# Stage projections in column tiles of 32 outputs and a second convolution in tiles of 32 by 64

## The chip, the cores and the metric

The kernel runs on one core of one Trainium2 chip. The metric is the time of one execution on the device in microseconds; it stood at 2982.66 us (median of three runs) before the change. Below, PE is TensorE, DVE is VectorE, ACT is ScalarE, POOL is GpSimd and SP is SyncE. A "pass" is one matmul record of the trace: an f32 matmul of this kernel is recorded as two.

## What is computed

The input is x with 2 images of 256 channels on 64 by 64 points, all in f32. Two layers follow each other. In short:

```python
# layer 0: full attention over 4096 tokens, 8 heads of 32, and a fusion with a mask
q, k, v = proj(Wq) / sqrt(32), proj(Wk), proj(Wv)
fuse = softmax(q @ k.T) @ v
hybrid = conv1x1(concat([x, fuse]), Wf) + bf
x = hybrid * m + x * (1 - m)
# layer 1: channel gate, window attention (8x8 windows, 4 heads of 64), two grouped 7x7 convolutions
a = relu(xp @ ca_w1 + ca_b1) @ ca_w2 + ca_b2
x = x * sigmoid(a)
q, k, v = split(windows(x) @ qkv_w + qkv_b)
x = x + (softmax(q @ k.T * 64**-0.5) @ v) @ out_w + out_b
x = shuffle(x, groups=4)
y = relu(bn(conv7x7(x, sa_w1, groups=64)))
y = bn(conv7x7(y, sa_w2, groups=64))
return x * sigmoid(y)
```

## The kernel before

A first part projects q, k and v and puts them into DRAM. Then `pipeline` runs, and nearly all of the time is spent there. One of two arms is taken at run time; the one in the profile has the suffix "a" on its tiles.

**The main loop** (lines 1177 to 1201) goes through 1024 slots: 2 images, 8 chunks of 512 queries, 2 groups of 4 heads, 32 blocks of 128 keys. A slot issues, in this order:

- `scores(i + 2)`: 8 matmuls of 32 rows by 64 columns on 512 queries (L633), into PSUM, and exponentials on ACT (L646);
- `products(i)`: 4 matmuls of 128 rows by 32 columns that accumulate the weighted values (L665), and on DVE one add of 128 x 2048 elements that sums the exponentials (L667). The first slot of a group of heads has no add;
- actions that fell due (`run_later`): at the end of a chunk come the denominators (L688, 128 rows by 32 columns), a reciprocal on DVE (L721), its spread over the heads on PE (L704) and a multiply (L724);
- at every fourth slot one piece of `stage`.

[...] The exponentials have 8 buffers, so PE and ACT can run ahead of DVE by some slots.

**The stage** (lines 728 to 989) does all the rest of a chunk of 512 tokens, in pieces that are spread over the slots of the next chunk. Its matmuls, with their form before the change (rows * columns of the array) and the recorded passes of one stage:

| line | what | form | passes |
|---|---|---|---|
| L739 | fusion of x and attention, 512 wide | 128*128 | 16 |
| L768 | first product of the channel gate, 256 wide | 128*64 | 8 |
| L782 | second product of the gate | 64*128 | 8 |
| L810 | query and key projections, twice | 128*128 | 8 each time |
| L844 | window scores, twice | 64*64 | 32 each time |
| L896 | value projection, 256 wide | 128*128 | 16 |
| L919, L938 | window probabilities transposed, window products | 64*64 | 64 each |
| L960 | output projection | 128*128 | 8 |

Between them ACT moves results out of PSUM and DVE does the multiplies and adds (L751, L753 after the fusion, L856 and L877 for the window softmax, L971 at the end). They stand in the same queues as the exponentials and the adds of the main loop. The stage of a chunk ends with its rows stored to DRAM for the convolutions.

**The convolutions** (`convolve`, lines 999 to 1151) run at the end, the first of them between the pieces of the last stage. They have 24 items: 16 "narrow" ones that treat one image (192 wide) and 8 "wide" ones that treat both (384 wide). For each item there is `conv1(k + 1)` (L1052, 28 matmuls of 128 rows by 32 columns), `conv2(k)` (L1076, 28 matmuls of 32 rows by 128 columns, in two PSUM pairs), two tanh on ACT (L1086) and a scaling (L1092) into `z`, which has two buffers, and `gate(k)`: one multiply on DVE (L1098) and 12 or 24 stores to the output (L1111). The stores go to POOL's and SP's queues in turn. For the items below 8 they all go to POOL once the last stage is done. The convolution weights live in the buffers of the exponentials, and SP loads them.

Of the kernel before, what the change touches and what calls it, by code (L numbers as in the profile page):

```python
# [17 lines left out]
B, C, H, W = 2, 256, 64, 64  # L18
# [19 lines left out]
KS, PAD = 7, 3  # L38
# [5 lines left out]
HALVES = (slice(0, 64), slice(64, 128))  # L44
# [12 lines left out]
def conv_seq_kernel(ctx: ExitStack, tc: tile.TileContext, a, out):  # L57
    nc = tc.nc
# [13 lines left out]
    def psum2(name):  # L72
        return ps["pair"].tile([P, 2, CH], F32, tag="s", name=name)
# [299 lines left out]
    with (  # L373
# [48 lines left out]
        for i, (b, c) in enumerate(chunks):  # L422
            load_chunk()
            x = xs0[i]
            sq = st0.tile([P, 2 * KC, CH], F32, tag="sq", name=f"sq_{b}_{c}")
            tops = st0.tile([P, 2 * KC, CH // 4], F32, tag="top4", name=f"top4_{b}_{c}")
            for n, w in (("q", wq), ("k", wk)):
                s = psum2(f"{n}0_{b}_{c}")
                for g in range(KC):
                    for kc in range(KC):  # L430
                        rhs = x[:, kc, :]
                        if n == "q":
# [5 lines left out]
                            start=(kc == 0),  # L438
                            stop=(kc == KC - 1),
# [26 lines left out]
        for i, (b, c) in enumerate(chunks):  # L466
            s = psum2(f"v0_{b}_{c}")
            sv = s.rearrange("p a (t o) -> p (a t) o", t=2)
            for m in range(4):
                for kc in range(KC):  # L470
# [4 lines left out]
                        start=(kc == 0),  # L475
                        stop=(kc == KC - 1),
# [21 lines left out]
            elif i == 2:  # L498
# [3 lines left out]
                for oc in range(KC):  # L502
                    for kc in range(KC):
# [4 lines left out]
                            start=(kc == 0),  # L508
                            stop=(kc == KC - 1),
# [10 lines left out]

    def pipeline(arm, shifted, pools):
        fp, xpool, gp, wp, avp, ctx_conv = pools
        cpool = ctx_conv.enter_context(tc.tile_pool(name=f"conv{arm}", bufs=1))
# [202 lines left out]
        def stage(b, c):  # L728
            x, f = xts.pop((b, c)), fts.pop((b, c))
# [6 lines left out]
            for half in range(2):  # L736
                for oc in range(KC):
                    for kc in range(KC * half, KC * half + KC):
                        nc.tensor.matmul(  # L739
                            s[:, oc, :],  # L740
                            wf[:, kc, oc * P : (oc + 1) * P],
                            f[:, kc - KC, :] if half else xw[kc],
                            start=(kc == 0),
                            stop=(kc == 2 * KC - 1),
                        )
# [19 lines left out]
            s = psum2(f"ca1{tag}")  # L765
            for kc in range(KC):
                for h in range(2):
                    nc.tensor.matmul(  # L768
                        s[64 * h : 64 * h + 64, 0, 0:half],
                        cw1[:, kc, :],  # L770
                        x1[:, kc, toks[h]],
                        start=(kc == 0),
                        stop=(kc == KC - 1),
                    )
# [4 lines left out]
            for oc in range(KC):  # L779
                for h in range(2):  # L780
                    r = slice(64 * h, 64 * h + 64)
# [4 lines left out]
                        start=True,  # L786
                        stop=True,
# [17 lines left out]
            def project(hc):  # L805
                s = psum2(f"qk{tag}_{hc}")
                for j in range(2):
                    o = (KC * j + hc) * P
                    for kc in range(KC):
                        nc.tensor.matmul(  # L810
                            s[:, j, :],
                            wqkv[:, kc, o : o + P],
                            u[:, kc, :],
                            start=(kc == 0),
                            stop=(kc == KC - 1),
                        )
                return s
# [56 lines left out]
            def normalise(hc):  # L874
                e, rs = es_[hc], sums[hc]
                nc.vector.reciprocal(rs, rs)
                nc.vector.tensor_mul(e, e, rs.unsqueeze(2).to_broadcast([P, 8, 64]))  # L877

            project_out(0, project(0))
            yield True  # L880
            window_scores(0)
            yield

            s = project(1)
            window_exp(0)
            project_out(1, s)
# [6 lines left out]
            sv = s.rearrange("p a (t o) -> p (a t) o", t=2)  # L893
            for t in range(4):
                for kc in range(KC):
                    nc.tensor.matmul(  # L896
                        sv[:, t, :],
                        u[:, kc, t * P : (t + 1) * P],
                        wqkv[:, kc, 2 * C : 3 * C],
                        start=(kc == 0),  # L900
                        stop=(kc == KC - 1),
                    )
# [9 lines left out]
            for hc in range(KC):  # L912
                for h in range(2):
                    for tt in range(2):
                        for odd in range(2):
                            for w in range(2):
                                r = slice(64 * w, 64 * w + 64)
# [5 lines left out]
                                    start=True,  # L923
                                    stop=True,
# [6 lines left out]
            o = s.rearrange("p w (a t q) -> p w a t q", a=KC, t=4)  # L931
            for hc in range(2):
                for t in range(4):
                    for w in range(2):
                        for h in range(2):
                            n = 2 * hc + h
                            r = slice(64 * w, 64 * w + 64)
# [4 lines left out]
                                start=True,  # L942
                                stop=True,
# [13 lines left out]
            y = gp.tile([P, KC, CH], F32, tag="t", name=f"y{tag}")  # L957
            for oc in range(KC):
                for kc in range(KC):
                    nc.tensor.matmul(  # L960
                        s[:, oc, :],
                        wo[:, kc, oc * P : (oc + 1) * P],
                        ots[kc],
                        start=(kc == 0),
                        stop=(kc == KC - 1),
                    )
# [32 lines left out]
        def convolve():  # L999
# [12 lines left out]
            weights = deque([*range(1, NU), 1])  # L1012
# [54 lines left out]
            def conv2(k):  # L1067
                u, images = items[k]
                n = nb * len(images)
                y = ys.pop(k)  # L1070
                w = ws[u][:, 32 * UW :].rearrange("p (m d) -> p d m", d=KS)
                tiles = [psum2(f"c2{arm}{k}_{hh}") for hh in range(2)]
                for d in range(KS):
                    for j in range(4):
                        r = slice(32 * j, 32 * j + 32)
                        nc.tensor.matmul(  # L1076
                            tiles[j // 2][:, j % 2, 0 : n * W],
                            w[r, d],
                            y[r, 0:n, d : d + W],
                            start=(d == 0),  # L1080
                            stop=(d == KS - 1),
                        )
                z = pool.tile([P, 4, B * nb * W], F32, tag="z", name=f"z{arm}{k}", bufs=2)
                z = z[:, :, 0 : n * W]
                for hh in range(2):
                    nc.scalar.activation(  # L1086
                        z[:, 2 * hh : 2 * hh + 2, :],
                        tiles[hh][:, :, 0 : n * W],
                        AF.Tanh,
                        scale=0.5,  # L1090
                    )
                nc.scalar.activation(z, z, AF.Copy, bias=0.25, scale=0.25)  # L1092
                return z.rearrange("p j (n x) -> p j n x", x=W)
# [42 lines left out]
            for k, (u, images) in enumerate(items):  # L1136
                while len(xs) <= k + 1 < len(items):
                    if not more():
                        yield
                conv1(k + 1)  # L1140
                yield
                more()
                z = conv2(k)
                yield
                more()
                gate(k, z)
                if xcs or k + 4 < EARLY:
                    load_rows(k + 4)

                if weights and (weights[0] <= 1 + EB or k >= EARLY):  # L1150
                    load_w(weights.popleft())
# [25 lines left out]
        for i, (b, c, g, m) in enumerate(slots):  # L1177
            now[0] = i
            if (b, c, g, m) == (B - 1, NCHUNK - 1, 0, 0):
                for _ in banded:  # L1180
                    pass
                conv = convolve()
                next(conv)
            if m % PB == 0:
                load_piece(i // PB + AHEAD)
            if g == KC - 1 and m == 0:
                nxt = (b, c + 1) if c + 1 < NCHUNK else (b + 1, 0)
                if nxt[0] < B:
                    load_q(*nxt)
            rest = scores(i + 2) if i + 2 < len(slots) else None  # L1190
            products(i)
            if rest:
                rest()
            if g == KC - 1 and m == NMB - 1:
                late = EB + 5 if (b, c) == (0, 0) else 0
                at(DN + 6 + late, lambda b=b, c=c: stages.append(stage(b, c)))
            run_later()
            if i % 5 == 1:
                next(banded, None)
            if i % 4 == 0:  # L1200
                run_stages()
# [20 lines left out]
    def arm(name, shifted):  # L1222
        with (
            tc.tile_pool(name=f"f{name}", bufs=1) as fp,
            tc.tile_pool(name=f"x{name}", bufs=1) as xpool,
            tc.tile_pool(name=f"g{name}", bufs=1) as gp,
            tc.tile_pool(name=f"w{name}", bufs=1) as wp,
            tc.tile_pool(name=f"av{name}", bufs=1, space=PSUM) as avp,
            ExitStack() as ctx_conv,
            tc.manual_schedule(),  # L1230
        ):
            pipeline(name, shifted, (fp, xpool, gp, wp, avp, ctx_conv))
# [71 lines left out]
```

## Time and profile before

| | us |
|---|---|
| median of three runs (2981.29 to 2983.53) | 2982.66 |
| the profiled execution | 2982.11 |
| its span, first to last instruction | 2980.3 |
| PE busy | 2942.5 |
| DVE busy | 2504.0 |
| ACT busy | 2474.1 |
| POOL busy | 267.1 |

The granted TensorE clock was 0.996 of full speed. The page's chain of waits, which is followed back from the last instruction, gives 87% of the span to PE, 34% of it to L633, 32% to L665; 6% to DVE; 2% each to the DMAs, ACT and POOL. The PE matmul groups that the change touches are busy for 118.4 us (L810), 116.7 us (L739, in two groups), 99.7 us (L1076), 59.5 us (L896), 59.2 us (L960) and 17.8 us (L768).

How to read the lines that follow: a group has the line of the source, the engine, the operation, what is written and read, the tile of the array (rows * columns) and the shape, then how many; behind the bar the busy time in us and the mean of one in ns, then the idle time of the engine before them and what ended it. A timeline line has the start and the duration in us first, and in brackets the idle time before it. Matmuls are pipelined and their ends are modelled, so the distance from one start to the next says more than a duration. A wait for several semaphores is put down to the one that came last.

### The profile page before, as it was taken

How to read it: one execution, taken by the hardware profiler on the slowest of the kernel's cores; microseconds unless marked ns; L12 is line 12 of the kernel's file. 1: busy time of each engine (PE TensorE's matmuls, PEld its weight loads, DVE VectorE, ACT ScalarE, POOL GpSimd, SP SyncE). 2: the span in 40 equal slices, each digit the busy share in tenths (PEclk: the TensorE clock that was granted, in tenths of full speed). 3: DMA queues.
4: the chain of work that ended last, by engine and by line, in shares of the span. 5: the costliest groups of instructions: out<-in, count | busy, mean ns of one | idle time of the engine just before them, and what ended most of it. 6: DMA issues, size and time to landing. Idle time of an engine off the chain costs nothing.

```text
span 2980.3 us, 77927 instructions
## 1 busy us (share of the span) xinstructions
PE 2942.5 (99%) x33674; PEld 928.1 (31%) x33674; DVE 2504.0 (84%) x1348; ACT 2474.1 (83%) x4151; POOL 267.1 (9%) x470
## 2 busy tenths in 40 slices
PE   9999999999999999999999999999999999999997
PEld 3551222222222222222222222222222222222775
DVE  4349999899999999999999999999999999999211
ACT  5569879898989898998989898989899898989433
POOL 8110000000000000000000000000000000000366
PEclk9999999999999999999999999999999999999998
DMA  8545322222242323232222223222323232322474
GB/s 247 198 166 171 119 70 52 78 67 70 54 80 63 81 63 69 72 75 70 65 70 67 70 53 74 63 74 62 68 74 73 68 73 68 101 66 86 128 215 103
DMA packets 224018, 267.12 MB, mean 90 GB/s; under 512 B 113384, under 2 KB 130108, under 8 KB 223408
## 3 DMA queue, kind: packets, MB, share of 16 engines
q1 hardware_dynamic: 200880, 231.47, 27.2%
q0 software_dynamic: 18416, 27.87, 4.6%
q8 instruction: 267, 4.37, 0.6%
q10 hardware_dynamic: 4368, 2.70, 0.3%
q14 instruction: 87, 0.71, 0.1%
HBM read 213.49 MB, written 66.13 MB: 94 GB/s over the span
## 4 chain that ended last, share of the span: by engine, by line
PE 87%; DVE 6%; DMA 2%; ACT 2%; POOL 2%; issue 1%; SPq 1%; DVEq 0%; ACTq 0%
PE sa L633 34%; PE ava L665 32%; DVE suma L667 5%; PE qka L810 4%; PE hya L739 4%; PE vwa L896 2%; PE opa L960 2%; PE v L471 2%; PE q L434 2%; POOL out_dram L1111 2%; PE k L434 1%; DMA out_dram<-za 1%; ACT ea L646 1%; PE sca L844 1%; PE rda L704 1%
## 5 line engine op out<-in xcount | busy, mean ns | idle before, releaser
L667 DVE TENSOR_TENSOR suma<-suma,ea 128x2048 f32<-128x2048 f32 x960 | 2198.8, 2290 | 87.9 <-ACT ea L646 1.4
L646 ACT ACTIVATE ea<-sa 128x512 f32<-128x512 f32 (+1 forms) x3072 | 2038.4, 745 | 74.3 <-PE sa L633 35.8
L633 PE MATMUL sa<-qa,ka 32*64 32x512 f32 x16384 | 1167.4, 613 | 1.5 <-ACT vst L479 1.2
L665 PE MATMUL ava<-ea,va 128*32 128x512 f32 x8192 | 1091.9, 605 | 1.3 <-ACT fa L675 0.3
L633 PEld LDWEIGHTS sa<-qa,ka 32*64 32x64 f32 x16384 | 251.4, 129 | 763.2 <-ACT ea L646 696.9
L665 PEld LDWEIGHTS ava<-ea,va 128*32 128x32 f32 x8192 | 161.6, 108 | 835.1 <-issue 806.2
L986 POOL DMA_DIRECT2D xs<-xo x94 | 65.9, 708 | 2524.0 <-DVE xo L971 2523.8
L1111 POOL DMA_DIRECT2D out_dram<-za x210 | 117.8, 569 | 74.3 <-DVE za L1098 51.3
L810 PE MATMUL qka<-ua,qkv_w 128*128 128x512 f32 x256 | 118.4, 605 | 0.0
L667 DVE TENSOR_TENSOR suma<-ea,ea 128x2048 f32<-128x2048 f32 x32 | 73.0, 2283 | 51.3 <-ACT ea L646 51.3
L1098 DVE TENSOR_TENSOR za<-za,xla 128x768 f32<-128x768 f32 (+1 forms) x16 | 21.7, 1359 | 108.2 <-ACT za L1092 60.1
L1076 PE MATMUL c2a<-yca,wa 32*128 32x192 f32 (+1 forms) x1344 | 99.7, 438 | 3.1 <-ACT za L1086 3.1
L453 DVE TENSOR_REDUCE top<-sq 128x512 f32<-128x2048 f32 x16 | 36.6, 2285 | 77.7 <-ACT sq L447 77.7
L1086 ACT ACTIVATE za<-c2a 128x384 f32<-128x384 f32 (+1 forms) x48 | 26.1, 595 | 90.8 <-DMA out_dram<-za 70.7
L747 ACT ACTIVATE ta<-hya,bf 128x512 f32<-128x512 f32 x32 | 20.3, 684 | 95.4 <-PE hya L739 89.2
L1076 PEld LDWEIGHTS c2a<-yca,wa 32*128 32x128 f32 x1344 | 90.9, 315 | 13.7 <-issue 9.6
L865 ACT ACTIVATE ewa<-ewa,mxwa 128x64 f32<-128x64 f32 x256 | 85.2, 346 | 1.5 <-DVE mxwa L856 1.5
L823 ACT ACTIVATE qka<-qka,qkv_b 128x512 f32<-128x512 f32 x64 | 40.5, 683 | 42.1 <-PE qka L810 41.7
L810 PEld LDWEIGHTS qka<-ua,qkv_w 128*128 128x128 f32 x256 | 46.0, 189 | 71.3 <-issue 46.1
L751 DVE TENSOR_TENSOR ta<-ta,mca 128x512 f32<-128x512 f32 x32 | 22.0, 688 | 54.5 <-ACT ta L747 54.5
L434 PE MATMUL q<-x,WqT 128*128 128x512 f32 x128 | 60.6, 617 | 5.1 <-DMA WqT<-in_WqT_dram 5.1
L896 PE MATMUL vwa<-qkv_w,ua 128*128 128x256 f32 x256 | 59.5, 386 | 0.0
(137 smaller groups left out, 1516.0 us busy)
## 6 DMA issues: line engine op xcount, KB each, us to landing
ka<-ks SPq DMA_DIRECT2D x256, 256.0 KB
va<-vs SPq DMA_DIRECT2D x256, 256.0 KB
wa<-ws SPq DMA_DIRECT2D x17, 896.0 KB
ws<-zeros SPq DMA_DIRECT2D x16, 896.0 KB
xs<-xo POOLq DMA_DIRECT2D x78, 140.0 KB, 6.3
xla<-xs SPq DMA_DIRECT2D x24, 420.0 KB
x<-in_x_dram SPq DMA_DIRECT2D x16, 512.0 KB
qs<-qst SPq DMA_DIRECT2D x16, 512.0 KB
```

The lines of the kernel that those rows point to most:

```text
L434: nc.tensor.matmul(s[:, g, :], w[:, kc, g * P : (g + 1) * P], rhs, start=(kc == 0), stop=(kc == KC - 1),)
L633: nc.tensor.matmul(heads[j][o], k[r, cols][:, o], q[r, g, :], start=True, stop=not shifted)
L646: nc.scalar.activation(e[:, h, :], tile, AF.Exp, scale=SCALE0)
L665: nc.tensor.matmul(av[r, :], v[:, m % PB, r], e[:, j, :], start=start, stop=stop)
L667: nc.vector.tensor_add(total, first[0] if m == 1 else total, e)
L739: nc.tensor.matmul(s[:, oc, :], wf[:, kc, oc * P : (oc + 1) * P], f[:, kc - KC, :] if half else xw[kc], start=(kc == 0), stop=(kc == 2 * K ...
L810: nc.tensor.matmul(s[:, j, :], wqkv[:, kc, o : o + P], u[:, kc, :], start=(kc == 0), stop=(kc == KC - 1),)
L865: nc.scalar.activation(e[:, n, :], e[:, n, :], AF.Exp, bias=mx[:, n : n + 1], accum_out=rs[:, n : n + 1],)
L896: nc.tensor.matmul(sv[:, t, :], u[:, kc, t * P : (t + 1) * P], wqkv[:, kc, 2 * C : 3 * C], start=(kc == 0), stop=(kc == KC - 1),)
L986: eng.dma_start(x_s[b, n, p + r0 : p + r1].rearrange("r g w -> g r w"), xo[64 * h : 64 * h + 64, oc, r0 - WS * c : r1 - WS * c, :],)
L1076: nc.tensor.matmul(tiles[j // 2][:, j % 2, 0 : n * W], w[r, d], y[r, 0:n, d : d + W], start=(d == 0), stop=(d == KS - 1),)
L1111: engines[stores % len(engines)].dma_start(dst[b, i, r0:r1, UG * u : UG * u + UG, :], z[p + r0 : p + r1, :, nb * m + n, :],)
```

## The change

Six matmul sites change, and nothing else does. A new helper splits the weights (the stationary operand) into tiles of 32 columns, and with them the output rows in PSUM; each tile streams the same x. It replaces the matmul call in the fusion (L739), the first gate product (L768), the projections (L810, L896) and the output projection (L960). In the second convolution each matmul of 32 rows by 128 columns becomes two of 32 rows by 64 columns; `HALVES` is the pair of slices 0 to 64 and 64 to 128. The elements that are multiplied and the order in which each output accumulates stay as they are.

```diff
+    def by_columns(out, weights, x, start, stop):
+        for o in range(0, weights.shape[-1], 32):
+            nc.tensor.matmul(
+                out[o : o + 32], weights[:, o : o + 32], x, start=start, stop=stop
+            )
...
-                        nc.tensor.matmul(
+                        by_columns(
                             s[:, oc, :],
                             wf[:, kc, oc * P : (oc + 1) * P],
                             f[:, kc - KC, :] if half else xw[kc],
...
-                    nc.tensor.matmul(
+                    by_columns(
                         s[64 * h : 64 * h + 64, 0, 0:half],
                         cw1[:, kc, :],
                         x1[:, kc, toks[h]],
...
-                        nc.tensor.matmul(
+                        by_columns(
                             s[:, j, :],
                             wqkv[:, kc, o : o + P],
                             u[:, kc, :],
...
-                    nc.tensor.matmul(
+                    by_columns(
                         sv[:, t, :],
                         u[:, kc, t * P : (t + 1) * P],
                         wqkv[:, kc, 2 * C : 3 * C],
...
-                    nc.tensor.matmul(
+                    by_columns(
                         s[:, oc, :],
                         wo[:, kc, oc * P : (oc + 1) * P],
                         ots[kc],
...
-                        nc.tensor.matmul(
-                            tiles[j // 2][:, j % 2, 0 : n * W],
-                            w[r, d],
-                            y[r, 0:n, d : d + W],
-                            start=(d == 0),
-                            stop=(d == KS - 1),
-                        )
+                        for o in HALVES:
+                            nc.tensor.matmul(
+                                tiles[j // 2][o, j % 2, 0 : n * W],
+                                w[r, d, o],
+                                y[r, 0:n, d : d + W],
+                                start=(d == 0),
+                                stop=(d == KS - 1),
+                            )
```

## The prediction

> **What bounds the kernel now.** I read the page first: busy shares, then the costliest groups.
>
> ```profile
> span 2980.3 us, 77927 instructions
> PE 2942.5 (99%) x33674; PEld 928.1 (31%) x33674; DVE 2504.0 (84%) x1348; ACT 2474.1 (83%) x4151; POOL 267.1 (9%) x470
> L667 DVE TENSOR_TENSOR suma<-suma,ea 128x2048 f32<-128x2048 f32 x960 | 2198.8, 2290 | 87.9 <-ACT ea L646 1.4
> L1076 PE MATMUL c2a<-yca,wa 32*128 32x192 f32 (+1 forms) x1344 | 99.7, 438 | 3.1 <-ACT za L1086 3.1
> ```
>
> PE is busy for 99%, but its ends are modelled, so I count from start to start. The second thing to see is VectorE: one softmax add takes 2.29 us, more than the PE needs for a slot. The timeline of PE around two stage pieces gives all prices:
>
> ```profile
> 1479.13 1.06 PE L665 MATMUL ava<-ea,va 128*32 128x512 f32 x8
> 1480.01 1.93 PE L688 MATMUL dna<-suma,keysum 128*32 128x128 f32 x64
> 1481.87 1.11 PE L633 MATMUL sa<-qa,ka 32*64 32x512 f32 x16
> ...
> 1534.45 1.06 PE L665 MATMUL ava<-ea,va 128*32 128x512 f32 x8
> 1535.44 3.70 PE L810 MATMUL qka<-ua,qkv_w 128*128 128x512 f32 x8
> 1539.08 1.11 PE L633 MATMUL sa<-qa,ka 32*64 32x512 f32 x16
> 1540.12 1.06 PE L665 MATMUL ava<-ea,va 128*32 128x512 f32 x8
> 1541.12 1.11 PE L633 MATMUL sa<-qa,ka 32*64 32x512 f32 x16
> ```
>
> A slot is 1.04 us of scores (tiles 32*64) and 1.00 us of products (128*32): 2.04 us. The products take 1.00 us before a group in another tile shape (1540.12 to 1541.12), and 0.88 us before the denominators, which have the same shape (1479.13 to 1480.01). So a change of shape costs about 0.115 us. An f32 matmul is two recorded passes; eight passes of L810 take 3.64 us, sixteen of L739 7.07 us (1501.82 to 1508.89), so a full-array pass is 0.429 us and a piece has 0.21 us of fixed cost.
>
> The timeline of weight loads at the start of L739 shows half of that cost: the second pass comes 0.54 us after the first (1501.82), the third 0.43 us after the second.
>
> ```profile
> 1502.36 0.19 PEld L739 LDWEIGHTS hya<-xa,WfT 128*128 128x128 f32 x1 [0.24 <-issue]
> 1502.79 0.19 PEld L739 LDWEIGHTS hya<-xa,WfT 128*128 128x128 f32 x1 [0.24 <-issue]
> ```
>
> Then VectorE's timeline in one chunk period (161.5 us), for who waits for whom:
>
> ```profile
> 1509.71 0.69 DVE L751 TENSOR_TENSOR ta<-ta,mca 128x512 f32<-128x512 f32 x1 [3.51 <-ACT ta L747]
> 1549.22 0.69 DVE L856 TENSOR_REDUCE mxwa<-ewa 128x8 f32<-128x512 f32 x1 [0.17 <-ACT ewa L852]
> 1552.14 16.67 DVE L667 TENSOR_TENSOR suma<-suma,ea 128x2048 f32<-128x2048 f32 x7
> 1569.81 0.69 DVE L856 TENSOR_REDUCE mxwa<-ewa 128x8 f32<-128x512 f32 x1 [1.00 <-ACT ewa L852]
> ```
>
> and PE's at the one place where it waits for VectorE:
>
> ```profile
> 1648.36 0.56 PE L704 MATMUL rda<-inva,spread_h 32*64 32x128 f32 x12 [0.82 <-DVE inva L721]
> ```
>
> Seven adds in 16.67 us are 2.39 us each: VectorE is slower than PE's slot and idles only three times a period. Call these points A (DVE waits for the fusion, 3.51 us), B (waits for the second window scores, 1.00 us) and C (PE waits for VectorE's reciprocal of L721, 0.5 to 0.8 us). From A to B, and from C to the next A, PE decides; from B to C VectorE runs without a real gap, and what PE wins there only lengthens its wait at C.
>
> [...] the denominators' 64 passes take 1.86 us; less one change of shape that is 0.109 us for a round of four 32-column tiles streaming 128 elements, beside 0.107 us that 0.429 us for 512 elements gives.
>
> **The change, part by part.** *Stage pieces.* Each full-array pass becomes four passes of 32 columns that run side by side, so the streaming time stays: 16 rounds of 0.429 for L739, 8 for each L810 and for L960, 16 of 0.216 for L896 (256 wide), 4 of 0.216 for L768, which already had two column tiles and two passes per tile. PE gets some 2,800 more matmul passes and as many loads, hidden: eight instructions fall in 0.43 us, and L919 issues 64 of each in 1.09 us. What goes is the change of shape ahead of the piece, since the products before it have shape 128*32 too (0.115 us), and the exposed first load (about 0.09 us net). The change towards the scores behind it remains. So L739, each L810, L896 and L960 win 0.20 us, L768 0.15 us (it had 64-column loads). Whole stage: 1.15 us.
>
> Which of this arrives? Between A and B lie L768 and both L810: 0.55 us. At B VectorE's 1.00 us gap shrinks to about 0.6 and still exists, so all 0.55 arrives; 14 periods (chunks 2 to 15) give 7.7 us. Between C and A lies L739: 0.20 us, 13 periods, 2.6 us. L896 and L960 lie between B and C: 0.40 us per period turns into a longer wait at C and counts nothing. Were VectorE not in the way, they would add 13 x 0.4 = 5 us. Chunk 0 has no stage; the fusion of the first stage falls where VectorE is the bound (adds every 2.39 us, full exp buffers). The rest of that stage and the fusion after it precede the first real wait A: 4 x 0.20 + 0.20 = 1.0 us. After the last B nothing of VectorE is late, so L896 and L960 count: 0.4 us. Sum in the loop: 11.7 us. The last stage runs among convolutions, where first-convolution neighbours have shape 128*32 as well; with the same prices about 1.0 us.
>
> *Second convolution.* The tail's timeline gives 3.51 us for 56 passes 192 wide and 4.90 us for 384 wide. The difference is 0.099 us a round, but 192 elements at L810's rate need 0.161 us. So the narrow form waits for its loads of 128 columns: a round is 0.24 us. The first convolution (128*32) takes 2.48 and 4.76 us for its 14 rounds: 0.166 and 0.329 us a round with 0.15 fixed. With 64 columns there are eight loads per round, [...] The nearest row is L633, also 32*64: its 16 passes take 1.04 us, less a change of shape 0.925, which is two rounds and 0.07 us, [...] so all eight load side by side. [...] 1.0 us won for each of 16 narrow items; and 14 x 0.329 + 0.17 = 4.77: 0.13 for each of 8 wide ones. Bounds: nothing (loads still 0.24 us a round), or 1.1 us.
>
> What arrives in the tail: items 0 to 4 lie where PE decides: 5.0 us. Then the page's chain leaves PE:
>
> ```profile
> 2822.55 7.29 POOL L1111 DMA_DIRECT2D out_dram<-za  x13 [3.40 <-DVE za L1098]
> ...
> 2836.37 12.74 POOL L1111 DMA_DIRECT2D out_dram<-za  x23 [0.37 <-DMA out_dram<-za]
> ...
> 2852.85 0.87 ACT L1086 ACTIVATE za<-c2a 128x384 f32<-128x384 f32 x2 [5.25 <-DMA out_dram<-za]
> ```
>
> Items 4 to 7 put all 12 stores on POOL, 0.56 us each, 6.7 us an item, beside 5.97 us of PE now and 5.0 then. Their tanh waits for a z buffer, and PE stalls on PSUM behind it. Until the tanh of item 10 nothing more is won. Items 11 to 14 then catch up by some 3 us (1.1 each for three would be the most), and the wide items add 1.0. The end, from item 21's stores on POOL, only shifts. Tail: 5 + 3 + 1 = 9 us.
>
> Sum: 11.7 + 1.0 + 9 = 21.7 us. The profiled execution took 2982.1 us (span 2980.3 and 1.8 around it), which is 0.6 under the median of the runs. 2982.1 - 21.7 = 2960.4; I forecast 2960.5 us, 0.7% faster.
>
> **Rivals.**
> 1. *The loop wins, the tail doesn't*: the 64-column loads still set a 0.24 us round, or PE, which now issues 336 passes and loads in 5 us there instead of 224 in 6, runs short of instructions, or stores hold all of it. For it: 70% DMA share in the tail and tanh waits for stores. Against: L633's side by side loads. Then 2982.1 - 12.7 = 2969.4.
> 2. *The tail wins, the loop doesn't*: VectorE takes all, because A and B move with it. For it: busy 151 of 161 us with 0.1 us between adds. Against: gaps of 3.51 and 1.00 us at A and B. Then 2982.1 - 9 - 1 = 2972.
> 3. *Slower*: four tiles that stream the same rows at the same time. L665 and L688 stream four different slices; only L633 shows two tiles on one slice, no four. If the reads collide, every round of the stage grows; L739's first half reads x with a stride on top. Rounds that count: 36 a period in 15 periods, 540; 21.7 us / 540 = 40 ns a round is the point from which it decides. If a round became 0.534 us, as with an exposed load, the counting rounds lose 540 x 0.105 = 57 us, and the 24 rounds from B to C lose 2.5 us less the 0.9 us that the wait at C absorbs, 13 times: 21 us. Then about 2982 + 78 - 22 = 3038.
>
> **How the numbers follow.** Forecast 0.65 (2953 to 2966: the low end if L896 and L960 arrive too, the high end if the tail gives half), rival 1 0.17, rival 2 0.08, slower 0.10. The range 2953 to 2972 holds the first three up to their centres and leaves the slow case out. About 0.2%, 6 us, can be told from no change: faster 0.87, same 0.04, slower 0.09.
>
> **What would show it.** L810 in 3.5 us and the products ahead of it in 0.88; the wait at C about 0.4 us longer, B about 0.4 us shorter, the period 160.8 us; narrow second convolutions in 2.5 us; items 4 to 9 of the tail still paced by POOL. Rounds above 0.47 us in L739 or L810 would make it wrong, as would a period under 160.3 (VectorE not in the way).

## The result, and the profile after

The changed kernel takes 2972.26 us (median of 6 runs, 2967.86 to 2976.29), the kernel before 2982.86 us (6 runs, 2981.29 to 2983.53). The ratio is 0.9962, with a 95% interval of 0.9952 to 0.9973. The change is worth some 10.6 us, half of the 21.7 that were forecast. The profiled execution of the changed kernel took 2973.0 us, its span is 2971.2.

In the code of the changed kernel, every line of the stage and of the convolutions stands 6 or 7 lines lower (L739 would be L745), and all six pieces that use the new helper are recorded under its one line, L525. The second convolution is L1083, its tanh L1093, its stores L1118.

These lines of the page after show the busy shares, the queue that brings instructions (packets, MB, share of the DMA engines), the softmax adds and the second convolution.

```profile
span 2971.2 us, 86307 instructions
PE 2914.8 (98%) x37834; PEld 858.0 (29%) x37834; DVE 2502.5 (84%) x1348; ACT 2469.1 (83%) x4151; POOL 267.1 (9%) x470
q8 instruction: 299, 4.90, 0.7%
L673 DVE TENSOR_TENSOR suma<-suma,ea 128x2048 f32<-128x2048 f32 x960 | 2198.7, 2290 | 87.9 <-DVE suma L673 1.4
L1083 PE MATMUL c2a<-yca,wa 32*64 32x192 f32 (+1 forms) x2688 | 89.0, 398 | 11.7 <-ACT za L1093 9.0
```

PE's busy time is 27.7 us less, yet only 9.1 us of span are gone. The row of the second convolution already shows a part of the answer: its busy time fell from 99.7 to 89.0 us, its idle time rose from 3.1 to 11.7 us.

PE's timeline around one projection in the loop:

```profile
1527.81 1.06 PE L671 MATMUL ava<-ea,va 128*32 128x512 f32 x8
1528.69 3.62 PE L525 MATMUL qka<-ua,qkv_w 128*32 128x512 f32 x32
1532.24 1.11 PE L639 MATMUL sa<-qa,ka 32*64 32x512 f32 x16
```

From start to start the products ahead of the piece take 0.88 us, the piece 3.55 us. Before it was 0.99 and 3.64. VectorE's timeline at the points A (L757) and B (L862), and PE's at C:

```profile
1503.26 0.69 DVE L757 TENSOR_TENSOR ta<-ta,mca 128x512 f32<-128x512 f32 x1 [3.34 <-ACT ta L753]
...
1562.78 0.69 DVE L862 TENSOR_REDUCE mxwa<-ewa 128x8 f32<-128x512 f32 x1 [0.67 <-ACT ewa L858]
```

```profile
1641.32 0.56 PE L710 MATMUL rda<-inva,spread_h 32*64 32x128 f32 x12 [1.22 <-DVE inva L727]
```

A and B became shorter (3.51 to 3.34, 1.00 to 0.67 us), C longer (0.82 to 1.22 us).

Then the convolutions, in PE's timeline:

```profile
2801.65 2.65 PE L1083 MATMUL c2a<-yca,wa 32*64 32x192 f32 x112
2804.23 2.54 PE L1058 MATMUL c1a<-xea,wa 128*32 128x192 f32 x56
...
2818.61 2.24 PE L1083 MATMUL c2a<-yca,wa 32*64 32x192 f32 x86
2822.03 0.95 PE L1083 MATMUL c2a<-yca,wa 32*64 32x192 f32 x26 [1.18 <-issue]
...
2837.01 0.61 PE L1083 MATMUL c2a<-yca,wa 32*64 32x192 f32 x8
2841.63 4.76 PE L1083 MATMUL c2a<-yca,wa 32*64 32x192 f32 x104 [4.01 <-ACT za L1093]
```

The first pair shows the second convolution as it was meant: 2.58 us from start to start. The second pair is a new sight. The group breaks off after 86 of 112 passes and goes on 1.18 us later, and no semaphore ended that gap ("issue"). The third pair is item 10: after its first 8 passes PE stands for 4 us. In the kernel before, a narrow item took 3.50 us, and PE stood for 0.56 us at item 10:

```profile
2846.09 3.57 PE L1076 MATMUL c2a<-yca,wa 32*128 32x192 f32 x56
2849.59 2.54 PE L1052 MATMUL c1a<-xla,wa 128*32 128x192 f32 x56
2852.06 0.78 PE L1076 MATMUL c2a<-yca,wa 32*128 32x192 f32 x4
2853.39 3.56 PE L1076 MATMUL c2a<-yca,wa 32*128 32x192 f32 x52 [0.56 <-ACT za L1086]
```

In the changed kernel it waits for a PSUM buffer that the tanh of the item before has to empty. That tanh had itself been waiting for 7.89 us, as ACT's timeline shows, for a z buffer whose stores were not done:

```profile
2841.09 0.87 ACT L1093 ACTIVATE za<-c2a 128x384 f32<-128x384 f32 x2 [7.89 <-DMA out_dram<-za]
```

When PE starts again, its 104 passes take 4.70 us to the next group's start. The windows of the changed kernel show why (us, then busy time and count of PE, PEld, DVE, ACT and POOL, the granted clock, the DMA share, GB/s):

```profile
2833.00:2837.00 4.00, 4.00 (x136) 3.48 (x121) 0.88 (x1) 0.20 (x1) 3.01 (x7) 1.00 0.29 60
2837.00:2841.50 4.50, 0.62 (x12) 0.33 (x8) 0.00 (x0) 0.41 (x2) 3.81 (x7) 0.87 0.84 266
2841.50:2844.50 3.00, 2.87 (x72) 2.52 (x80) 0.96 (x1) 1.61 (x4) 0.38 (x1) 0.50 0.32 119
2844.50:2847.50 3.00, 3.00 (x62) 1.92 (x52) 0.00 (x0) 1.49 (x3) 2.99 (x6) 0.56 0.34 70
```

During the stall POOL is busy with stores for 3.81 of 4.5 us, and after it the granted clock is 0.50. By the trace's records of the granted clock, it fell 2.7 us into the wait of 4.01 us in the changed kernel. In the kernel before it fell 1.5 us into a wait of 2.54 us ahead of the last group, and in the loop, from 410.9 to 414.3 us, behind two waits of 0.98 and 0.68 us. These runs give no length of wait from which it falls: at the same place in its loop the changed kernel waits for 1.18 and 0.69 us, and its clock stays at 1.00. The waits of the kernel before:

```profile
408.79 0.65 PE L768 MATMUL ca1a<-x1a,ca_w 128*64 128x256 f32 x4 [0.98 <-DVE x1a L753]
410.11 0.65 PE L768 MATMUL ca1a<-x1a,ca_w 128*64 128x256 f32 x4 [0.68 <-DVE x1a L753]
410.70 1.95 PE L633 MATMUL sa<-qa,ka 32*64 32x512 f32 x16
412.57 1.88 PE L665 MATMUL ava<-ea,va 128*32 128x512 f32 x8
...
2961.62 4.87 PE L1076 MATMUL c2a<-yca,wa 32*128 32x192 f32 x52 [2.54 <-ACT za L1086]
```

To split the time I take the start of the last exponential of the main loop as the loop's end; all that follows is the tail. In the profiled executions:

| | loop ends | tail | span |
|---|---|---|---|
| before | 2753.4 | 226.9 | 2980.3 |
| after | 2740.8 | 230.4 | 2971.2 |
| after, profiled once more | 2740.8 | 231.3 | 2972.1 |

In these executions the loop ends 12.6 us earlier, and the tail, which was to win 9 us and 1 us of the last stage, takes 3.5 us longer. Some 1.6 us of the 12.6 are not the change's: in the lines above, the half clock in the loop of the kernel before stretched scores and products from 2.04 to 3.68 us, and no other profile of these runs has it at that place. That leaves about 11 us for the loop. Beside medians that are 10.6 us apart, the tail by this account won nothing of its 10 us.

### The profile page after: what moved, and what is told of

Read it like the earlier page. It is cut to its first block, busy times and chain, and to the rows that moved or that the text cites. A ratio compares the mean times of both kernels' runs of the same rounds, so it can differ in the third digit from the quotient of the medians.

```text
span 2971.2 us, 86307 instructions
## 1 busy us (share of the span) xinstructions
PE 2914.8 (98%) x37834; PEld 858.0 (29%) x37834; DVE 2502.5 (84%) x1348; ACT 2469.1 (83%) x4151; POOL 267.1 (9%) x470
## 4 chain that ended last, share of the span: by engine, by line
PE 86%; DVE 7%; DMA 2%; ACT 2%; POOL 1%; issue 1%; SPq 0%; DVEq 0%; ACTq 0%; POOLq 0%
PE sa L639 33%; PE ava L671 31%; DVE suma L673 5%; PE qka L525 4%; PE hya L525 4%; PE q L434 2%; PE k L434 2%; PE v L471 2%; PE vwa L525 2%; PE opa L525 2%; POOL out_dram L1118 1%; DMA out_dram<-za 1%; ACT ea L652 1%; PE dna L694 1%; PE sca L850 1%
## 5 line engine op out<-in xcount | busy, mean ns | idle before, releaser
L1118 POOL DMA_DIRECT2D out_dram<-za x210 | 117.8, 569 | 76.9 <-DVE za L1105 53.1
L1105 DVE TENSOR_TENSOR za<-za,xla 128x768 f32<-128x768 f32 (+1 forms) x16 | 21.7, 1359 | 112.3 <-ACT za L1099 59.8
L525 PE MATMUL qka<-ua,qkv_w 128*32 128x512 f32 x1024 | 115.8, 592 | 0.2 <-PE c2a L1083 0.2
L1083 PE MATMUL c2a<-yca,wa 32*64 32x192 f32 (+1 forms) x2688 | 89.0, 398 | 11.7 <-ACT za L1093 9.0
L1093 ACT ACTIVATE za<-c2a 128x384 f32<-128x384 f32 (+1 forms) x48 | 26.2, 596 | 89.0 <-DMA out_dram<-za 68.2
L1083 PEld LDWEIGHTS c2a<-yca,wa 32*64 32x64 f32 x2688 | 68.0, 193 | 33.0 <-issue 13.6
L757 DVE TENSOR_TENSOR ta<-ta,mca 128x512 f32<-128x512 f32 x32 | 22.0, 688 | 50.3 <-ACT ta L753 50.3
L1058 PE MATMUL c1a<-xla,wa 128*32 128x192 f32 (+1 forms) x896 | 60.1, 413 | 3.3 <-issue 1.6
L525 PE MATMUL vwa<-qkv_w,ua 128*32 128x256 f32 x1024 | 58.2, 379 | 0.0
```

Source lines behind the costliest of these rows:

```text
L525: nc.tensor.matmul(out[o : o + 32], weights[:, o : o + 32], x, start=start, stop=stop)
L1058: nc.tensor.matmul(s[32 * j : 32 * j + 32, 0 : n * W], w[:, j, d, :], xs[k][:, 0:n, j, d : d + W], start=(d == 0), stop=(d == KS - 1),)
L1083: nc.tensor.matmul(tiles[j // 2][o, j % 2, 0 : n * W], w[r, d, o], y[r, 0:n, d : d + W], start=(d == 0), stop=(d == KS - 1),)
L1118: engines[stores % len(engines)].dma_start(dst[b, i, r0:r1, UG * u : UG * u + UG, :], z[p + r0 : p + r1, :, nb * m + n, :],)
```

## The experiments

Each median is set against that of the kernel before on the same chip (2984.29 to 2985.03 us there). The theory to be tested was that the loop wins by the stage alone and between A, B and C as forecast, and that the tail's gain is taken back by waits; its rivals were that the pieces between B and C count too (the chain of waits gives PE 86%), and that the split convolution gains nothing in itself.

**One half of the change each.** One kernel has the stage in column tiles and the old second convolution. The other is the reverse, which is this edit of the kernel before:

```diff
-                        nc.tensor.matmul(
-                            tiles[j // 2][:, j % 2, 0 : n * W],
-                            w[r, d],
...
+                        for o in HALVES:
+                            nc.tensor.matmul(
+                                tiles[j // 2][o, j % 2, 0 : n * W],
+                                w[r, d, o],
...
```

> The stage in column tiles, the second convolution as before. Theory A (the loop's gain is real and only shifts what follows; the narrow second convolution as such brings nothing because the tail is short of instructions and of stores): the loop ends about 13 us earlier and the tail takes its 227 us as before, so about 2970 us, no slower than the changed kernel, with no stall of PE inside a matmul group in the tail. Theory B (the split of the second convolution still wins some us in the tail): 2974 to 2980, slower than the changed kernel.

> The second convolution in 32*64 tiles, the stage as before. The prediction's price: 9 us less, 2974. Theory A: the loop is the same, the tail gets its 1 us per narrow item and gives nearly all of it back to PE waiting for instructions and to the stores on GpSimd: 2979 to 2986, with stalls inside groups of L1076 and L1052 that no semaphore explains.

The stage alone took 2975.22 us against 2984.29, ratio 0.9972 [0.996, 0.9983], 9.1 us won. That lies in the range of theory B, but the interval overlaps that of the whole change, so these runs don't tell the two apart. The second convolution alone took 2983.38, ratio 0.9997 [0.9989, 1.0005], which is not to be told from nothing, although a narrow item that nothing disturbs takes 2.57 us, as in the full change. So nearly all that the whole change brings comes from the stage. The loop of the second kernel has the old period (161.52 us) and yet ends at 2752.0, 1.4 us earlier than that of the kernel before: it lacks the half clock there. Its tail is 229.1.

**Which pieces of the stage count.** First the helper serves only the value and output projections (L896, L960), which lie between B and C; then only the fusion, the first gate product and the query and key projections:

```diff
# value and output only, against the kernel before
-                    nc.tensor.matmul(
+                    by_columns(
                         sv[:, t, :],
...
-                    nc.tensor.matmul(
+                    by_columns(
                         s[:, oc, :],
                         wo[:, kc, oc * P : (oc + 1) * P],
...
# fusion, gate, query and key only, against the kernel before
-                        nc.tensor.matmul(
+                        by_columns(
                             s[:, oc, :],
                             wf[:, kc, oc * P : (oc + 1) * P],
...
-                    nc.tensor.matmul(
+                    by_columns(
                         s[64 * h : 64 * h + 64, 0, 0:half],
...
-                        nc.tensor.matmul(
+                        by_columns(
                             s[:, j, :],
...
```

> Only the value projection and the output projection in column tiles (between the points B and C). Theory A (VectorE decides from B to C): PE wins 0.4 us per chunk and waits 0.4 us longer at C, the period stays 161.5, the whole 0.4 to 1 us faster: 2982. Rival (PE decides all through, as the chain of waits says): 0.4 us in each of 16 stages, 2976.5.

> Only the fusion, the first gate product and the query and key projections in column tiles (C to A and A to B). Theory A: the period falls to 160.8 us as with all of them, the wait at C does not grow, some 12 us faster: 2971. Rival (gain in proportion to PE time saved, 0.75 of 1.15 us): two thirds of the gain of the stage alone, about 2974.5.

The first took 2983.48 us (0.9998 [0.9989, 1.0006]), the second 2978.39 (0.9979 [0.9971, 0.9987]). The loop decides it more sharply than the totals: its period is 161.52 us in the first, just that of the kernel before (161.51), and 160.79 in the second, just that of the full change (160.78). Where the time of L896 and L960 went stands in the waits of PE, over the whole run, for VectorE at C (us in total, times, longest). Before, with value and output only, and with the others only:

```profile
PE rda L704 <- DVE inva L721: 6.7, 12, 0.8
```

```profile
PE rda L710 <- DVE inva L727: 10.6, 11, 1.2
```

```profile
PE rda L710 <- DVE inva L727: 6.3, 11, 0.8
```

What PE wins between B and C it stands waiting for at C. From the start of the last product to that of the spread (L704) most chunks show 1.06 us before and 1.46 us with value and output only, and the two pieces were priced at 0.40.

The total of the second kernel was a miss. Some 12 us had been expected and 5.9 came, about the two thirds of the stage's 9.1 us that the rival named. The period speaks against that rival, and the rest is lost in the tail: its loop ended at 2743.6, 9.8 us earlier than that of the kernel before, but its tail took 231.7 us. With the second convolution as before, PE stood there for 4.80 us at item 10:

```profile
2848.35 4.33 PE L1082 MATMUL c2a<-yca,wa 32*128 32x192 f32 x52 [4.80 <-ACT za L1092]
```

So the long wait at item 10 does not need the split convolution.

**What goes when the tile changes.** Here the helper makes tiles of 64 columns in place of 32, so that the form differs from that of the products (128*32). The second convolution is the old one:

```diff
-        for o in range(0, weights.shape[-1], 32):
+        for o in range(0, weights.shape[-1], 64):
             nc.tensor.matmul(
-                out[o : o + 32], weights[:, o : o + 32], x, start=start, stop=stop
+                out[o : o + 64], weights[:, o : o + 64], x, start=start, stop=stop
             )
```

> The stage alone, in column tiles of 64 outputs in place of 32; the first gate product and the second convolution are as before. The form 128*64 differs from that of the products. Theory A (what goes is the change of shape ahead of the piece, 0.115 us, and a part of the first load): the products ahead of a piece still take 1.00 us, each piece wins some 0.05 us from a first load of half the columns, the period falls from 161.5 to about 161.35, the whole 1 to 3 us faster than before. Rival (the tiling as such, by loads of other tiles beside a stream, is what wins): period 160.8 to 160.9 as with 32 columns, products unchanged.

The period is 161.39 us: without the match of the forms 0.12 us are left of the 0.73 us a period that the 32-column tiles win. PE's timeline of this kernel:

```profile
1534.10 1.06 PE L671 MATMUL ava<-ea,va 128*32 128x512 f32 x8
1535.09 3.65 PE L525 MATMUL qka<-ua,qkv_w 128*64 128x512 f32 x16
1538.67 1.11 PE L639 MATMUL sa<-qa,ka 32*64 32x512 f32 x16
```

The piece is 3.58 us, close to the 3.55 of the 32-column tiles, but the products ahead of it take 0.99 us again. The sum of the two, 4.57 us, is 0.06 under the kernel before; with 32 columns it is 0.20 under. The whole was slower than before, 2988.92 us against 2984.83 (1.0012 [1.0005, 1.0018]), which I had not expected. The profiled run puts it in the tail (233.1 us), where PE waits for tanh for 4.6 us in all (3.1 before) and once for 2.4 us for convolution weights. What makes this tail longer than that of the other kernels was not settled.

**More instructions for the same work.** Here the second convolution of the changed kernel runs in four tiles of 32 columns:

```diff
-                        for o in HALVES:
+                        for o in (slice(q, q + 32) for q in range(0, P, 32)):
```

> The changed kernel with the second convolution in tiles of 32 by 32, four per former matmul: 448 matmul passes and loads in a narrow item in place of 224, the same streaming. Theory A (PE's instruction supply limits the tail; a fetch brings 256 instructions and comes every 3.5 us or more): a narrow item needs 560 instructions with its first convolution, 2.2 fetches, so 7 us or more in place of 5; the tail grows by 15 to 40 us: 2987 to 3012, with many stalls that no semaphore explains, each ending 1.2 to 1.7 us after the end of a packet on the instruction queue. Theory B (the stalls come from stores and PSUM alone): within 3 us of the changed kernel, 2970 to 2976.

It took 3031.82 us, 47 us over the kernel before (1.0155 [1.0138, 1.0172]), more than expected. PE's timeline of one item:

```profile
2821.01 2.38 PE L1083 MATMUL c2a<-yca,wa 32*32 32x192 f32 x119
2825.64 2.26 PE L1083 MATMUL c2a<-yca,wa 32*32 32x192 f32 x105 [2.25 <-issue]
```

The waits of PE in the tail of this kernel, then of the changed one, then of the kernel before (us, times, longest; the kernel before has no line that ends in "issue"):

```profile
PE c2a L1083 <- issue: 21.7, 17, 2.8
PE c1a L1058 <- issue: 8.4, 4, 2.9
```

```profile
PE c2a L1083 <- ACT za L1093: 9.0, 3, 4.0
PE c1a L1058 <- issue: 3.1, 2, 1.6
PE c2a L1083 <- issue: 2.7, 4, 1.2
```

```profile
PE c2a L1076 <- ACT za L1086: 3.1, 2, 2.5
```

PE stands without waiting for a semaphore, at an arbitrary pass of a group, and the more often the more instructions the same work has. The reading that fits is that PE has nothing to execute, and the packets of the instruction queue in the trace support it. A packet is 16 KB. The quarters have 5376 instructions more on their page than the changed kernel (91683 and 86307) and 21 more packets (320 and 299), which is 256 instructions for each. In the tail of the changed kernel the packets start 3.3 us or more apart. There the packet that matters ended at 2820.76 and PE resumed at 2822.03; other pairs are 2796.02 and 2797.40, 2861.05 and 2862.66. In these two kernels all such stalls of 0.6 us or more ended 1.2 to 1.6 us after the end of a packet. Counted from the start of the last pass ahead to that of the first one behind, such stalls are 0 before, 6 in the changed kernel (7.8 us in all) and 22 with quarters (38.7 us; one of them is at L944, outside the lines above). With quarters the granted clock was also 0.50 for 23.9 us of the tail. With the stage alone there were two (4.8 us), both in the loop, and a stretch at half clock followed the second, so its loop ends at 2745.2 and not at 2740.8. Three more of the kernels with the stage in column tiles had one stall of 1.5 to 1.8 us in the loop, each just behind the denominators. So the tail is not the only place. The dose is shown; what decides when a packet is asked for and why it takes so long is not.

**Stores out of the way.** The second suspect is the chain of stores, z buffer, tanh and PSUM. The rule that gives the early items' stores to POOL alone is dropped, so that they go to POOL's and SP's queues in turn: in the changed kernel, in the one with the stage alone, and in the kernel before.

```diff
-                elif staged and k < EARLY:
-                    engines = (nc.gpsimd,)
```

> The changed kernel with the stores of the items below 8 always spread over GpSimd's and SyncE's queues. Theory A (48 stores on GpSimd alone hold items 4 to 9): the 4 us stall of PE at item 10 and the clock that falls with it go, tanh of items 5 to 10 waits less, 4 to 7 us faster than the changed kernel: 2965 to 2969. Rival (instruction supply or DMA traffic sets the tail in any case): no more than 1 us faster, or slower since the loads of rows stand behind the stores on SyncE.

> The stage in column tiles, the second convolution as before, and the stores of the items below 8 spread over GpSimd's and SyncE's queues. Theory A (with the stores out of the way the split of the second convolution is worth the 5 us by which it shortens items 0 to 4, and some of what items 5 to 13 save, less the stalls for instructions): the loop's 13 us arrive, the tail stays near the 229 us of the kernel before with the same stores, 2970 to 2973, some 4 us slower than the changed kernel with both queues. Rival (the split is worth nothing even then): 2966 to 2968.

> The kernel before with the same edit to the stores. Theory A: GpSimd's stores hold PE there only by half a microsecond at item 10, so 0 to 2 us faster than before. Rival (they cost as much there as in the changed kernel): 4 us or more faster.

| edit on | us | kernel before | ratio |
|---|---|---|---|
| changed kernel | 2967.15 | 2984.83 | 0.9940 [0.9923, 0.9956] |
| stage alone | 2972.67 | 2985.03 | 0.9960 [0.9946, 0.9974] |
| kernel before | 2984.81 | 2984.83 | 1.0003 [0.9994, 1.0011] |

The same edit is worth nothing on the kernel before and 5 us or more on the changed one (2967.15 against its 2972.26 and 2972.97 on other chips). In the kernel before it moves a wait of PE: 2.6 us at 2837.2 in place of the 2.54 us ahead of the last group. So what this order of the stores costs depends on the kernel around it. The stage alone gains some 3 us by the edit (12.4 won against 9.1, on two chips). With both queues the split convolution is worth some 5 us (17.7 won against 12.4, on two chips), not the 0.9 that it brought by itself.

The changed kernel, measured again beside the second of these, took 2972.97 us (0.9957 [0.9943, 0.997]). Its profile has the same marks: 10.7 us of waits for tanh (6.4 the longest), 4.2 us of stalls for instructions and half clock for 10.2 us from 2839.0.

> The changed kernel itself, for a comparison on one chip. Its profile again shows the loop's end 12 to 13 us earlier than before, stalls inside groups that no semaphore explains, and at least one fall of TensorE's clock in the middle of the tail: 2969 to 2976.

**A third z buffer.** The direct cure for a tanh that waits for a buffer, first with both queues, then with the stores as the change has them:

```diff
-                z = pool.tile([P, 4, B * nb * W], F32, tag="z", name=f"z{arm}{k}", bufs=2)
+                z = pool.tile([P, 4, B * nb * W], F32, tag="z", name=f"z{arm}{k}", bufs=3)
```

> The changed kernel with the stores on both queues and three z buffers in place of two. Theory A (what is left of the stall at item 6 is its tanh waiting for the stores of item 4, which land late beside four row loads): PE's 2.3 us wait there and the clock's fall with it go, and so does the 4 us wait before the last item: 2958 to 2963. Rival (the instruction supply or the stores' own rate sets the tail): within 2 us of the kernel with both queues, 2965 to 2969.

> The changed kernel with three z buffers, the stores of items below 8 still on GpSimd alone. Theory A (a third buffer lets tanh and PE run on while GpSimd works off its stores): the 4 us stall at item 10 and the fall of the clock go, 5 to 9 us faster than the changed kernel, 2963 to 2967. Rival (GpSimd's 27 us of stores for items 4 to 7 only move the stall to a later item): at most 2 us faster.

With both queues it took 2965.78 us (2963.85 to 2970.6) against 2984.69, ratio 0.9940 [0.9926, 0.9954]: hardly better than without the buffer, and short of what was expected. With the stores left alone it took 2963.22 us (2962.32 to 2965.06), ratio 0.9927 [0.9913, 0.9941], as expected. This is the best version; it beats the kernel before by 21.5 us and the change by some 10. PE's waits in its tail:

```profile
PE c1a L1058 <- DMA out_dram<-za: 3.0, 1, 3.0
PE c2a L1083 <- issue: 2.4, 3, 1.6
PE c1a L1058 <- issue: 2.1, 2, 1.2
PE c2a L1083 <- ACT za L1093: 0.7, 2, 0.5
```

The wait for tanh has gone from 9.0 to 0.7 us, and its tail is 219.9 us, 7.0 under that of the kernel before. The waits for instructions remain (4.5 us), and so does one stretch at half clock, 3.4 us from 2854.8, where the wait of 3.0 us in the first line stands. Why both queues with three buffers are not better still is open: the two intervals overlap. A third buffer in the kernel before was not tried, so how much of these 21.5 us it would bring there is open too.

## Why the prediction was half right

**The loop: right in mechanism and size.** The products ahead of a piece and L810 came as priced (0.88 us; 3.55 where 3.5 was said), and so did the shift at A, B and C: B 0.33 us shorter where 0.4 was said, C 0.40 us longer where 0.4 was said, the period 160.78 where 160.8 was said. The separate runs of the two sides of B show that VectorE rules from B to C and PE elsewhere. The forecast sum was 11.7 us. The trace gives 12.6, and about 11 without the half clock in the loop of the kernel before. That lies in chunk 1, where 2.25 us were won, against 1.3 in chunk 2 and some 0.74 in each later one. I do not build on the last microsecond: up to the end of the first chunk alone, profiles of kernels with the same code there differ by almost 2 us.

**No collision of the four tiles.** Rival 3 needed 40 ns more for a round; L810 became shorter. The rival in which VectorE takes all falls with the gap that B still has. That the loads of four column tiles, which share all rows, cost nothing beside the stream is carried by the traces: the 64 passes of the denominators take 1.86 us with 64 loads that are recorded at 110 ns each, and the piece of L810, with 32 loads in place of 8, takes 3.55 us in place of 3.64.

**The second convolution: right price, gain not kept.** A narrow item takes 2.58 us and a wide one 4.80 (2.5 and 4.77 forecast). From the trace before, L633, in the same form, takes 1.04 us, two rounds of 0.429 and 0.18 more; 14 rounds of 0.166 with that 0.18 give the 2.5, and 14 of 0.329 some 4.8. Less the 0.18, the 2.58 us are 0.17 us a round in place of 0.24. That the loads had set the 0.24 is the author's reading; the mean load is recorded at 315 ns with 128 columns and at 193 with 64. PE's work in the tail is 16 x 0.93 + 8 x 0.10 = 15.7 us less, besides 0.7 us of the last stage, where 1.0 was said.

**The step that failed** is the tail's sum, "5 + 3 + 1 = 9 us". Its first term, items 0 to 4 with "5.0 us", came as 2.6 to 3.4: the gates of items 2 to 4 stand that much earlier after the loop's end, and two of the six instruction stalls lie there (from 2791.4 and 2795.6). "Until the tanh of item 10 nothing more is won" was too kind, since by item 9 the gain was gone (0.8 us later than before). The second term, "Items 11 to 14 then catch up by some 3 us", came with the wrong sign: item 13 stands 4.0 us later than before. I had taken the stores' pace as a floor at which PE's time is merely lost. But the wait reaches PE: at item 10 of the kernel before PE stood for 0.56 us, in the changed one for 4.01 us, and the granted clock fell with it. That the wait grows because PE arrives earlier is argued and not shown, since the kernel with fusion, gate, query and key only had 4.80 us there with the old second convolution. The 104 and 56 passes behind it took about 2.7 us more than at full clock, and the last group of the second convolution, after another wait of 4.01 us, 1.8 us more. In the kernel before, the last group had lost some 1.5 us in the same way.

Put together for the tail of these two executions, each group from start to start against the same group where nothing disturbs it: 16.4 us were won. Given back were 9.3 us in the groups with stalls for instructions, 1.4 in a wait for an input, and 8.3 more in waits for tanh and the half clock behind them (14.6 against 6.3 before), 19.0 in all. That leaves a loss of 2.6 us, where the tail lost 3.5; the rest was not placed.

The case that came is closest to rival 1 ("runs short of instructions, or stores hold all of it"), which would have given 2969.4. I set L633's side-by-side loads against it (16 of them, recorded at 129 ns each, lie within 0.23 us). They speak on the price of a round, and the round was right; they say nothing on supply or stores. The page before did show 70% DMA share and tanh that waits for stores there, and I read it only as lost gain.

## What to carry to other kernels

Give neighbouring groups on TensorE the same tile form: here that took the products ahead of a piece from 0.99 to 0.88 us, the stage in that form won some 0.3%, and it counts only between the points where PE decides. When an engine is made faster in front of a chain of buffers, price what the chain does with an engine that arrives early, down to its clock, and give the buffers in the same step. And splitting a matmul into more instructions is not free: PE had 6 stalls for instructions (7.8 us) with the second convolution in two tiles and 22 (38.7 us) with four. Count the instructions per microsecond.

## What had not been expected of the hardware

- PE seems to run out of instructions: six times in a tail that issues 336 passes and loads in 5 us, never before, and 22 times with four tiles, 38.7 us together. In the changed kernel the DMA engines are busy for 0.53 of the tail and 0.29 of the loop; whether that slows the packets was not tested.
- A stall of 4.01 us costs more than itself: the granted clock fell to 0.50 for 6.8 us, and PE was at work for most of them. Shorter waits had it too: 2.54 us in the kernel before, 2.39 us with the stage alone, where the scores behind it took 1.94 us in place of 1.04.
- The same edit of the store queues is worth nothing before the change and 5 us after it.
- Tiles of 128*64 are as quick as 128*32 within a piece (3.58 and 3.55 us), but keep the 0.11 us at its start.
